# Three moves at the border between layer 1 and the recurrence of a four-layer graph network

## The chip, the cores and the metric

The kernel runs on one core of one Trainium2 chip. The metric is the device time of one execution in microseconds (us): the median of several runs. Below, PE is the matmul engine (TensorE), DVE is VectorE, ACT is ScalarE, POOL is GpSimd and SP is SyncE. SP computes nothing: it issues DMA transfers, one queue for all of them. POOL computes and issues transfers as well, in a queue of its own. Each engine works through its instructions in the order in which they stand.

## The reference, cut to what matters

Sixteen graphs of 1024 nodes with 256 features pass four layers, each of the form `x = x + layer(relu(layernorm(x)), adj)`. Layer 0 is an attention layer, layer 1 a graph convolution, layer 2 a gated recurrence over the nodes, layer 3 a two-layer perceptron on sums over neighbours. Layer 2 is what the change leads up to:

```python
def step(h, i):
    x = jnp.take(h_e, i, axis=1)
    row = jnp.take(norm_adjT, i, axis=1)
    x_par = jnp.einsum('bj,bjd->bd', row, h)
    iou = x @ W_ioux.T + b_ioux + x_par @ W_iouh.T + b_iouh
    r, z = jnp.split(iou, 2, axis=1)
    r, z = (jax.nn.sigmoid(r), jax.nn.sigmoid(z))
    hc = jnp.tanh(x @ W_coux.T + b_coux + x_par * r @ W_couh.T + b_couh)
    h_new = z * x_par + (1.0 - z) * hc
    h = jax.lax.dynamic_update_slice(h, h_new[:, None, :], (0, i, 0))
    return (h, None)
h_out, _ = jax.lax.scan(step, h_e, jnp.arange(n))
```

Node `i` takes the states of all other nodes, those before it already new. So the 1024 steps are sequential in principle. There are two biases for each gate, one with `x` and one with `x_par`; only their sum matters.

## The kernel before, in words

**Layers 0 and 1** (`layers_0_1`) run in one loop over the 16 graphs (line 639). Iteration `i` does layer 0 of graph `i` and layer 1 of graph `i - 1`, and in small helper functions (`a0` to `a6`, `d0` to `d6`), called between the big matrix products, everything that must be ready for the next graph: loads (`load_x`, `get`), stores (`keep`), moments, copies. For all five engines the order of the instructions is the order in which they are written (`tc.manual_schedule`, line 267). At the end of an iteration `late_norm` (line 791) makes `he`, the normalised input of layer 2, and stores it on SP; the next iteration begins with SP's load of `x` for the graph after next.

**Jobs** prepare layer 2 during these iterations, one for each graph (class `Job`, line 485). Inside a tile of 128 nodes the nodes are put into an order in which groups of 16 depend little on one another. A job loads the adjacency near the diagonal and the first column of tiles (`load`: `ad` at line 504 and `ab` at 506, both issued on SP), masks them (`mask`, POOL, lines 517 and 519), turns `he` into feature-major order (`turn`, stored to `heT_d` by POOL at 541), sums the first tile's contributions (`first`, PE line 547), puts the adjacency into the new order (`order`, PE 558 and 560, stored to `near_d` and `next_d` by POOL at 568 and 569), and stores the sums (`base`, to `base_d`, 578). `scale` (524, 525) multiplies by inverse degrees on POOL. The jobs of graphs 14 and 15 come after the loop (lines 806 to 835). Job 15 uses the same tile `ad` as job 13, so its load has to wait for job 13's `order`.

**The recurrence** (`layer_2`, line 852) goes over eight tiles `t` of 128 nodes and in each over eight groups `s` of 16. On PE, DVE, ACT and POOL the written order holds there too (line 1195). Before the first group it needs: the weights `wx` and `wh`, the biases, `he` of tile 0 in feature-major order for all graphs (`load_he`, line 989, issued on SP at 993 in pieces for graphs 0 to 13, 14 and 15), the base sums `bxt` (line 1202), and the reordered adjacency rows of the group, which POOL gathers from `near_d` with an indirect DMA (`Sub.__init__`, line 1008). `Sub.behind` and `Sub.own` spread the gathered rows by products on POOL (1024, 1015).

`Gates(he, s)` (line 1028) copies the group's input to `hs` on POOL (two instructions, line 1034) and makes tasks of the three gate products with `wx` (PE, 1043), whose results get the bias on their way out of PSUM (ACT 1051 for the first, DVE 1048 for the others). For group 0 the tasks are run before the loop. For group 1 they go to the list `todo` of group 0 and are put between its steps by `fill`, which compares the tasks' estimated costs with the share of the step that is over. Two of the three gates come ahead of the first product of the recurrence (`round_`, PE line 1097). Behind them in the list are the base sums of the next tile (`base_tasks`; PE 928, their loads on SP at 895 and 901, their mask on POOL at 906), which need POOL once more.

In the setup ahead of the loop the order on POOL is therefore: the two copies for group 0, the two gathers, four products, and only then, inside group 0, the two copies for group 1 and the gathers of the next group:

```python
he = load_he(0)
gx = Gates(he, 0)
sub = Sub(0, 0)
```

```python
if s == 0:
    gx_next = gx_ahead or Gates(he, 1)
```

For later tiles the copies for group 1 are already made in the last group of the tile before (line 1315), as `gx_ahead`.

**Layer 3** follows, graph by graph (`layer_3`).

Of the kernel before, what the change touches and what calls it, by code (L numbers as in the profile page):

```python
# [9 lines left out]
F32 = mybir.dt.float32  # L10
# [6 lines left out]
P = 128  # L17
B, N, D, H = 16, 1024, 256, 1024
NT = N // P
DC = D // P  # L20
# [22 lines left out]
def gnn_stack(ctx: ExitStack, tc: tile.TileContext, a: dict, out: bass.AP):  # L43
    nc = tc.nc
    const = ctx.enter_context(tc.tile_pool(name="const", bufs=1))
# [25 lines left out]
    table = [const.tile([P, G2, NT, NS], mybir.dt.int32, name=f"table{k}") for k in range(2)]  # L71
    place = const.tile([P, NT * B], F32, name="place")
    dinv = const.tile([P, B, NT], F32, name="dinv")

    def rows(ap):
        return ap.rearrange("(t p) d -> p t d", p=P)
# [187 lines left out]
    def layers_0_1():  # L264
        with ExitStack() as st:
            ET = mybir.EngineType
            st.enter_context(tc.manual_schedule(engines={ET.PE, ET.DVE, ET.Activation, ET.Pool, ET.SP}))
            wp = st.enter_context(tc.tile_pool(name="w01", bufs=1))
# [4 lines left out]
            x, q, h1, h2, g, dis, mean, rs_of, ags = {}, {}, {}, {}, {}, {}, {}, {}, {}  # L273
# [52 lines left out]
            class Moments:  # L326
# [7 lines left out]
                def first(self, tiles):  # L334
                    junk = psum.tile([P, 512], F32, name="pt")[:, :D]
                    for t in tiles:
                        nc.scalar.activation(junk, self.x[:, t], AF.Identity, accum_out=self.sum[:, t : t + 1])
# [13 lines left out]
            def normed(h, x, shift, scale, tiles):  # L351
                for t in tiles:
                    nc.scalar.activation(h[:, t], x[:, t], AF.Relu, bias=shift[:, t : t + 1], scale=scale[:, t : t + 1])
# [235 lines left out]
            def side(us):  # L589
                while later:  # L590
                    later.popleft()()
                left[0] += us * 1.25
                while left[0] > 0:
                    cost = next(math, None)
                    if cost is None:
                        break
                    left[0] -= cost
                left[0] = min(left[0], 0.0)
# [38 lines left out]
            job15 = Job(15, {"hT": "h1", "ao": "q"})  # L637

            for i in range(B):
# [162 lines left out]
                if ahead:  # L802
                    left_of, first, second = combos(q[i + 1])
                    first()
                side(5.0 if run_a else 3.0)
            h2[14] = big.tile([P, NT, D], F32, name="h2", bufs=2)
            normed(h2[14], x[14], m2.shift, m2.rs, all_)
            nc.sync.dma_start(rows(he_d[14]), h2[14])
# [10 lines left out]
            run_b.order()  # L819
            run_b.base()  # L820
            job14.scale()
            h2[15] = big.tile([P, NT, D], F32, name="h2", bufs=2)
            normed(h2[15], x[15], shift, rs, all_)
            nc.sync.dma_start(rows(he_d[15]), h2[15])
            job15.load()
            job14.first()
            job14.turn()
            job14.base()
# [23 lines left out]
    def layer_2(shared, early):  # L852
        with ExitStack() as st:
            wp = st.enter_context(tc.tile_pool(name="w2", bufs=1, reuse_waits="tile"))
# [6 lines left out]
                nc.sync.dma_start(t[:, :, 2 * D :], a[co].rearrange("(c p) e -> p c e", p=P))  # L861
            load_w(wx, "W_iouxT", "W_couxT")

            bias = wp.tile([P, 3, DC], F32, name="bias")
            bias2 = wp.tile([P, 3, DC], F32, name="bias2")
            with nc.allow_non_contiguous_dma(reason="biases, once"):
                for t, io, co in ((bias, "b_ioux", "b_coux"), (bias2, "b_iouh", "b_couh")):
                    nc.sync.dma_start(t[:, :2].rearrange("p q c -> p (q c)"), a[io].rearrange("(k p) -> p k", p=P))
                    nc.sync.dma_start(t[:, 2], a[co].rearrange("(c p) -> p c", p=P))
            nc.vector.tensor_add(bias, bias, bias2)  # L870

            own = wp.tile([P, GB], F32, name="own")
            nc.vector.tensor_reduce(own, ident.rearrange("p (b j) -> p b j", b=GB), AX.X, ALU.add)
# [115 lines left out]
            def load_he(t):  # L989
                he = big.tile([P, DC, B, P], F32, name="he")  # L990
                for b0, b1 in parts if t == 0 else ((0, B),):
                    for c in range(DC):
                        nc.sync.dma_start(he[:, c, b0:b1], heT_d[b0:b1, :, c, t * P : (t + 1) * P].rearrange("b p i -> p b i"))
                return he
# [199 lines left out]

            with tc.manual_schedule(engines={mybir.EngineType.PE, mybir.EngineType.DVE, mybir.EngineType.Activation, mybir.EngineType.Pool}):
                he = load_he(0)
                gx = Gates(he, 0)
                sub = Sub(0, 0)
                bxt = shared.tile([P, DC, B, P], F32, name="bxt")
                for b0, b1 in parts:  # L1200
# [9 lines left out]
                gx.seed_r()  # L1210
                gx.seed_zc()

                near = gx_ahead = None
                behind = []
                for t in range(NT):
                    if t == NT - 1:
# [9 lines left out]
                    for s in range(NS):  # L1226
# [15 lines left out]
                        else:  # L1242
# [8 lines left out]
                            while any(lists):  # L1251
                                i = max(range(2), key=lambda i: len(lists[i]) / max(sizes[i], 1))
                                if s < 5 and share and 6 <= len(todo) < 10:

                                    i = 1
# [15 lines left out]
                        for c in range(DC):  # L1271
                            to = x[:, c].rearrange("p (b i) -> p b i", b=B)
# [16 lines left out]
                        for k, (i0, i1) in enumerate(steps):  # L1289
# [19 lines left out]
                            if k == 0:  # L1309
                                gx_now, gx = gx, gx_next  # L1310
                                if s > 0 and sub_next:
                                    nc.gpsimd.tensor_copy(tick, rx[:, DC - 1].rearrange("p b i -> p (b i)")[:, :1] if K > 1
                                                          else rx[:, DC - 1, :1])
                                    gx = Gates(he if ahead[0] == t else he_next, ahead[1])
                                    gx_ahead = Gates(he_next, 1) if s + 1 == NS else None
# [28 lines left out]
                        near = None  # L1344
                        if s + 1 < NS:
                            near = psum.tile([P, DC, G2 * GR], F32, name="pa")
# [5 lines left out]
                        elif t + 1 < NT:  # L1352
                            next_block(h, sub.bd, 0, False)
                            near = pnx
                            behind = last_tasks(t + 1, bxt_next)
                            bxt, he = bxt_next, he_next
# [67 lines left out]
    def layer_3(shared, x, hn, at, h, eye):  # L1424
        with ExitStack() as st:
# [274 lines left out]
            for b in range(B):  # L1700
# [27 lines left out]
                for k in range(2, 4):  # L1728
                    eps_of((b + 2) * NQ + k)

    layers_0_1()
    with tc.tile_pool(name="shared", bufs=2, reuse_waits="tile") as shared:
        x, hn, at, h = {}, {}, [], {}
        with tc.tile_pool(name="first3", bufs=1, reuse_waits="tile") as first:
            eye = layer_2(shared, early_3(shared, first, x, hn, at, h))
            layer_3(shared, x, hn, at, h, eye)
# [55 lines left out]
```

## Time and profile before

| | |
|---|---|
| median of 3 runs | 4305.25 us (4303.75 to 4311.17) |
| the profiled execution, own time | 4306.4 us |
| its span, first to last instruction | 4304.6 us |
| mean granted clock of PE | 0.982 |
| DMA traffic | 744.72 MB, 173 GB/s on average |
| layers 0 and 1 | until about 1320 us |
| the border: last jobs, setup of the recurrence | about 1320 to 1380 us |
| biases on SP at the border (868, 869) | 1327.66 to 1336.04 us |
| loads of `he` for tile 0 on SP (993) | issued from 1336.34 us |
| first gates on PE (1043) | from 1354.82 us |
| first product of the recurrence on PE (1097) | 1379.63 us |

The profile is of one execution. A line of the timeline gives start, duration, engine, source line, operation, what was written and read, and the number of instructions; in brackets stands the idle time of the engine ahead of the instruction and the one that ended it. PEld are PE's weight loads. SPq is SP's DMA queue: its times are those of issuing a transfer, not of the transfer. "DMA share" is the mean busy share of the 16 DMA engines; with many transfers at once it can read a little above 1.

### The profile page before, as it was taken

How to read it: one execution, taken by the hardware profiler on the slowest of the kernel's cores; microseconds unless marked ns; L12 is line 12 of the kernel's file. 1: busy time of each engine (PE TensorE's matmuls, PEld its weight loads, DVE VectorE, ACT ScalarE, POOL GpSimd, SP SyncE). 2: the span in 40 equal slices, each digit the busy share in tenths (PEclk: the TensorE clock that was granted, in tenths of full speed). 3: DMA queues.
4: the chain of work that ended last, by engine and by line, in shares of the span. 5: the costliest groups of instructions: out<-in, count | busy, mean ns of one | idle time of the engine just before them, and what ended most of it. 6: DMA issues, size and time to landing. Idle time of an engine off the chain costs nothing. (4 is left out here: it accounts for less than half of the span.)

```text
span 4304.6 us, 56454 instructions
## 1 busy us (share of the span) xinstructions
PE 4045.7 (94%) x19307; PEld 2805.0 (65%) x19307; DVE 2677.6 (62%) x6293; ACT 1554.8 (36%) x3907; POOL 1643.0 (38%) x1740
## 2 busy tenths in 40 slices
PE   7999999999997999999999999998799999999998
PEld 3545455555555888888888888877466565665656
DVE  7888987578763434443444444454477777877776
ACT  3454545444432222222222222223233433333332
POOL 2232323434334333232333333333535446364552
PEclk9999999999999999999999999999799999999999
DMA  6666657998767363546364545441443434434320
GB/s 231 209 224 226 215 203 259 266 301 293 266 222 247 123 195 121 188 128 194 122 198 131 185 140 177 145 139 39 158 170 118 150 125 137 157 118 157 122 103 20
DMA packets 406702, 744.72 MB, mean 173 GB/s; under 512 B 75168, under 2 KB 325664, under 8 KB 365344
## 3 DMA queue, kind: packets, MB, share of 16 engines
q1 hardware_dynamic: 370976, 613.49, 41.8%
q0 software_dynamic: 26080, 109.21, 8.9%
q10 hardware_dynamic: 9216, 16.78, 1.1%
q8 instruction: 210, 3.44, 0.3%
q14 instruction: 220, 1.80, 0.1%
HBM read 538.85 MB, written 183.76 MB: 168 GB/s over the span
## 5 line engine op out<-in xcount | busy, mean ns | idle before, releaser
L86 POOL TENSOR_TENSOR rs<-rs_v,mhalf 128x8 f32<-128x8 f32 (+1 forms) x65 | 112.3, 1727 | 932.1 <-DVE rs_v L82 720.4
L928 PE MATMUL pf<-hb,ab 128*128 128x256 f32 x1568 | 416.7, 384 | 7.5 <-DMA hb<-hs_d 7.5
L1043 PE MATMUL pf<-hs,wx 128*128 128x256 f32 x1536 | 346.8, 382 | 15.5 <-POOL hs L1034 13.5
L1043 PEld LDWEIGHTS pf<-hs,wx 128*128 128x128 f32 x1536 | 292.9, 192 | 58.5 <-POOL hs L1034 14.6
L1342 POOL DMA_INDIRECT hs_d<-h,table x128 | 129.0, 1008 | 510.7 <-ACT gates L1051 451.1
L1570 POOL TENSOR_TENSOR ss<-ss,sq 128x512 f32<-128x512 f32 x224 | 298.9, 1350 | 22.8 <-ACT sq L1568 16.7
L928 PEld LDWEIGHTS pf<-hb,ab 128*128 128x128 f32 x1568 | 272.4, 191 | 45.9 <-issue 9.9
L418 PE MATMUL pmm<-w,ag 128*128 128x256 f32 x1024 | 244.9, 394 | 26.1 <-DVE x L421 12.5
L1048 DVE TENSOR_TENSOR gates<-pf,bias 128x512 f32<-128x512 f32 x128 | 88.4, 692 | 289.0 <-PE pf L1043 289.0
L1633 PEld LDWEIGHTS po<-w,hh 128*128 128x128 f32 x2048 | 239.0, 194 | 16.6 <-issue 11.0
L418 PEld LDWEIGHTS pmm<-w,ag 128*128 128x128 f32 x1024 | 197.1, 196 | 76.3 <-DVE x L421 28.5
L1633 PE MATMUL po<-w,hh 128*128 128x128 f32 x2048 | 243.1, 278 | 1.4 <-ACT hh L1616 0.7
L1079 PE MATMUL pf<-bd,h 128*128 128x384 f32 (+4 forms) x512 | 188.8, 458 | 38.1 <-DVE bxt L1082 31.0
L1568 ACT ACTIVATE sq<-hh 128x512 f32<-128x512 f32 x224 | 141.2, 631 | 197.9 <-POOL ss L1570 119.6
L1516 PE MATMUL ph<-bxt,hb 128*128 128x512 f32 x440 | 199.8, 600 | 3.2 <-ACT hb L1488 1.8
L1141 ACT ACTIVATE r<-pr 128x128 f32<-128x128 f32 (+2 forms) x256 | 57.9, 278 | 384.3 <-PE pr L1097 379.3
L1082 DVE TENSOR_TENSOR bxt<-bxt,pf 128x384 f32<-128x384 f32 (+4 forms) x256 | 127.8, 501 | 86.4 <-PE pf L1079 84.6
L1566 DVE SCALAR_TENSOR_TENSOR hh<-ph,b,u 128x512 f32<-128x512 f32 x192 | 141.2, 749 | 46.6 <-PE ph L1562 36.3
L1616 ACT ACTIVATE hh<-hh,rw 128x512 f32<-128x512 f32 x256 | 158.7, 708 | 24.3 <-DVE hh L1615 24.3
L1158 DVE TENSOR_TENSOR w<-w,hc 128x128 f32<-128x128 f32 (+2 forms) x256 | 75.5, 295 | 139.8 <-ACT hc L1157 139.8
L1615 DVE TENSOR_TENSOR hh<-hh,po 128x512 f32<-128x512 f32 x256 | 154.3, 679 | 2.9 <-PE po L1612 2.9
L345 ACT ACTIVATE pt<-x,m_neg 128x256 f32<-128x256 f32 x240 | 114.3, 476 | 108.6 <-DVE m_neg L340 102.3
(363 smaller groups left out, 9238.0 us busy)
## 6 DMA issues: line engine op xcount, KB each, us to landing
at<-in_quarters SPq DMA_DIRECT2D x94, 1024.0 KB, 10.9
t_d<-at SPq DMA_DIRECT2D x64, 1024.0 KB, 10.7
ab<-in_columns SPq DMA_DIRECT2D x127, 512.0 KB, 3.5
bxt<-t_d SPq DMA_DIRECT2D x42, 1024.0 KB, 4.9
bxt<-in_quarters SPq DMA_DIRECT2D x34, 1024.0 KB, 4.8
at<-at POOLq DMA_DIRECT2D x30, 1024.0 KB, 10.5
at<-t_d SPq DMA_DIRECT2D x22, 1024.0 KB, 4.8
pc<-in_own ACTq DMA_DIRECT2D x64, 256.0 KB, 7.2
```

The source lines that it names most:

```text
L418: nc.tensor.matmul(po[:, t - t0], ag[:, c, t * P : (t + 1) * P], w[:, c], start=c == 0, stop=c == DC - 1)
L928: nc.tensor.matmul(pb, ab[:, jts[k]], hb[:, jts[k]], start=k == 0, stop=k == len(jts) - 1)
L1043: nc.tensor.matmul(pg[:, e], wx[:, c, q * D + e * P : q * D + (e + 1) * P], self.hs[:, c], start=c == 0, stop=c == DC - 1)
L1079: nc.tensor.matmul(pf, h[:, g, c * P : (c + 1) * P], bd[:, g, b0 : b0 + n, S : S + far], start=True, stop=True)
L1342: nc.gpsimd.indirect_dma_start(out=hs_d[t][g][:, :], out_offset=row(1, g, t, s), in_=h[:, g], in_offset=None)
L1516: nc.tensor.matmul(pa, st[left][:, k], at[q % 6][:, k], start=onto is None and k == 0, stop=k == 3, skip_group_check=True)
L1566: behind3[:] = [nc.vector.scalar_tensor_tensor(hh[q][:, k], ph, b1[:, k : k + 1], u, op0=ALU.add, op1=ALU.add)]
L1568: nc.scalar.activation(sq, hh[q][:, k], AF.Square)
L1570: nc.gpsimd.tensor_tensor(ss[q], ss[q], sq, ALU.add)
L1615: nc.vector.tensor_mul(hh[q][:, k], hh[q][:, k], pr)
L1616: nc.scalar.activation(hh[q][:, k], hh[q][:, k], AF.Silu, scale=rw[:, k : k + 1])
L1633: nc.tensor.matmul(po[:, n], left[:, c, n * P : (n + 1) * P], right[:, c], start=onto is None and n == 0 and c == 0, stop=c == HH - 1, ski ...
```

## The change

Three things are moved; no arithmetic is added or removed.

- Job 15's two loads (`job15.load()`) stand ahead of graph 15's `normed` and the store of its `he`, instead of behind them.
- The four loads of biases and the addition that joins them move from the start of `layer_2` into layers 0 and 1: the loads to the end of iteration 3, the addition on DVE to the end of iteration 5. The two tiles, 6 numbers per partition each, now belong to the pool that lasts for the whole kernel, which lies below all others.
- `Gates(he, 1)`, that is the two POOL copies for group 1, is called directly behind `Gates(he, 0)` and so ahead of the gathers of `Sub(0, 0)`. Group 0 then takes it as `gx_ahead`; its matmuls stay where they were.

```diff
+    bias, bias2 = (const.tile([P, 3, DC], F32, name=name) for name in ("bias", "bias2"))
...
                 side(5.0 if run_a else 3.0)
+                if i == 3:
+                    with nc.allow_non_contiguous_dma(reason="biases, once"):
+                        for to, io, co in ((bias, "b_ioux", "b_coux"), (bias2, "b_iouh", "b_couh")):
+                            nc.sync.dma_start(to[:, :2].rearrange("p q c -> p (q c)"), a[io].rearrange("(k p) -> p k", p=P))
+                            nc.sync.dma_start(to[:, 2], a[co].rearrange("(c p) -> p c", p=P))
+                if i == 5:
+                    nc.vector.tensor_add(bias, bias, bias2)
...
             job14.scale()
+            job15.load()
             h2[15] = big.tile([P, NT, D], F32, name="h2", bufs=2)
             normed(h2[15], x[15], shift, rs, all_)
             nc.sync.dma_start(rows(he_d[15]), h2[15])
-            job15.load()
...
-            bias = wp.tile([P, 3, DC], F32, name="bias")
-            bias2 = wp.tile([P, 3, DC], F32, name="bias2")
-            with nc.allow_non_contiguous_dma(reason="biases, once"):
-                for t, io, co in ((bias, "b_ioux", "b_coux"), (bias2, "b_iouh", "b_couh")):
-                    nc.sync.dma_start(t[:, :2].rearrange("p q c -> p (q c)"), a[io].rearrange("(k p) -> p k", p=P))
-                    nc.sync.dma_start(t[:, 2], a[co].rearrange("(c p) -> p c", p=P))
-            nc.vector.tensor_add(bias, bias, bias2)
...
                 he = load_he(0)
-                gx = Gates(he, 0)
+                gx, gx_ahead = Gates(he, 0), Gates(he, 1)
                 sub = Sub(0, 0)
...
-                near = gx_ahead = None
+                near = None
```

## The prediction

> **What bounds the kernel now.** I began with the list of busy engines and the forty slices. TensorE (PE) is busy for 94% of the span, and its slices show 9 nearly everywhere. The exceptions include one 7 in the thirteenth slice, which is 1291 to 1399 us: the border between layers 0 and 1 and the recurrence. PE is the bound elsewhere, so only a pause of PE there can be won.
>
> ```profile
> PE 4045.7 (94%) x19307; PEld 2805.0 (65%) x19307; DVE 2677.6 (62%) x6293; ACT 1554.8 (36%) x3907; POOL 1643.0 (38%) x1740
> PE   7999999999997999999999999998799999999998
> ```
>
> Then I read the border in order of time, engine by engine. The columns are start, duration, engine and line, and in brackets the idle time before the instruction with what ended it.
>
> ```profile
> 1322.18 0.38 SPq L824 DMA_DIRECT2D he_d<-h  x1
> 1322.65 0.77 SPq L504 DMA_DIRECT2D ad<-in_near  x1
> 1323.47 1.38 SPq L506 DMA_DIRECT2D ab<-in_columns  x1
> ...
> 1337.10 5.61 PE L547 MATMUL pt<-h,ab 128*128 128x256 f32 x16 [6.24 <-POOL ab L519]
> ```
>
> Job 15's loads wait in SP's queue behind the store of `he` (L824), which waits for ACT. Job 15's first product then waits 6.24 us for `ab`. The tile that the loads write was free earlier: its last reader on PE began at 1318.54 and took 0.27 us.
>
> ```profile
> 1352.23 0.92 POOL L568 DMA_DIRECT2D near_d<-q  x1 [1.22 <-DVE own L873]
> 1354.37 0.81 POOL L1034 COPY hs<-he 128x256 f32<-128x256 f32 x2
> 1363.12 1.09 POOL L1008 DMA_INDIRECT aj<-near_d,table  x1 [7.93 <-DMA next_d<-q]
> 1369.18 3.75 POOL L1024 TENSOR_TENSOR bd<-aj,own 128x1024 f32<-128x1024 f32 x2 [3.69 <-DMA aj<-near_d,table]
> 1373.69 0.73 POOL L1034 COPY hs<-he 128x256 f32<-128x256 f32 x2
> 1354.82 7.02 PE L1043 MATMUL pf<-hs,wx 128*128 128x256 f32 x24 [3.82 <-POOL hs L1034]
> 1363.39 1.02 PE L1209 MATMUL pc<-wx,ident 128*128 128x512 f32 x2
> 1374.14 5.87 PE L1043 MATMUL pf<-hs,wx 128*128 128x256 f32 x16 [9.72 <-POOL hs L1034]
> ```
>
> The second `hs` copy needs only `he`, yet it stands on POOL behind the gather (L1008) and four products. PE waits 9.72 us for it, then runs two gates and starts the recurrence's first product (L1097) at 1379.63. Last, the DMA shares in stretches (the share and GB/s close each line):
>
> ```profile
> 1318.00:1338.00 20.00, 10.18 (x57) 7.94 (x58) 5.38 (x9) 6.93 (x14) 10.16 (x13) 0.90 1.04 388
> 1338.00:1340.00 2.00, 2.00 (x6) 1.55 (x6) 0.00 (x0) 0.00 (x0) 0.00 (x0) 0.50 0.84 132
> 1340.00:1364.00 24.00, 16.88 (x73) 12.13 (x71) 6.36 (x13) 4.26 (x8) 9.99 (x13) 0.91 1.11 328
> 1364.00:1383.00 19.00, 9.28 (x32) 7.47 (x32) 1.48 (x4) 2.64 (x4) 8.92 (x12) 0.73 1.10 317
> 1383.00:1391.00 8.00, 7.47 (x35) 6.24 (x34) 1.65 (x4) 1.95 (x6) 0.00 (x0) 1.00 0.01 2
> ```
>
> The DMA engines are full from 1318 to 1383. Reordering transfers here brings some forward and pushes others back; only bytes or time taken out of the stretch bring the last one forward.
>
> **What the Trainium skill says.** "DMA: Bandwidth & Descriptors", section "Queues, rings and completion order": an engine alternates between queues packet by packet. The trace agrees, since POOL's stores and SP's loads progress together here. The same page, "Rules for kernel authors": a load with a non-contiguous last dimension becomes one descriptor per element. The trace shows it: 1680 packets under 512 B from 1334 to 1340, for biases of 2 x (512 + 256) = 1536 elements. "TensorE: Matmul & The Clock Gate", Part 1, "What's actually happening": after some 3.4 us of idling PE runs at half clock for about as long. The trace has a granted clock of 0.50 from 1370 to 1378, after the 9.72 us wait.
>
> **The change, part by part.**
>
> **The copies ahead of the gather.** Two POOL copies (0.73 us together, no DMA) move past two gathers and four products. They fall into POOL's 7.93 us wait, so they delay the gather by nothing; without that cover it would be 0.73 us. PE's 9.72 us go. The two gates behind them then run warm: a later 24 of these matmuls take 5.34 us, so 16 take 3.6 instead of 5.87, 2.2 us less. Sum 11.9 us; L1097 could start at 1367.7. Next late would be its operands. `x` was ready at 1366.4. `wh` went out at 1359.5 to 1360.6, and the `ab` load right behind it landed 6.4 us after 1360.62, so `wh` is in by 1367.0. Neither binds.
>
> **Job 15's loads ahead of the store.** Two SP issues (0.77 and 1.38 us) go out at 1318.8 instead of 1322.65, 3.85 us earlier. The added wait, on PE, ends 3.4 us before the store's data is ready, so the store and `wx` behind it in SP's queue lose nothing. They also pass the 1.1 MB that POOL stored at 1320.0 to 1322.5. SP's and POOL's 3.0 MB then in flight at 388 GB/s take 7.8 us from about 1321, so `ab` lands near 1329.5, not 1336.7. L547 then waits only for the transposes ahead of it on PE, which end at 1330.9: it starts at about 1331.1, 6.0 us earlier, and warm (3.7 us as at 1319.5, not 5.61), 1.9 more. Job 15's stores on POOL go out 7.9 us earlier, at 1344.3, and the gather at about 1355.2.
> PE does not get 7.9 us. Its first gates need `he`, whose last pieces went out at about 1346 and landed in 6.2 to 7.4 us, at 1352.5. The transfers ahead of it are the same but for the biases (minus 1.7 us, below), and of the 1.94 MB that jobs 14 and 15 store, about half now runs ahead of it (0.95 MB at 360 GB/s, plus 2.6). I estimate `he` at 1353.3 and its copy at 1353.4, 1.0 us earlier than 1354.37. Bounds: 2.1 us later if all the stores pass it, 4.4 earlier if none does.
>
> **The biases.** SP loses four issues at the border, 0.57 + 4.34 + 0.55 + 2.78 = 8.2 us. That was hidden, as DMA was full throughout. What counts is the dip of 1338 to 1340: 2.0 us at 132 instead of 388 GB/s, worth 1.3 to 2.0 us; I take 1.7, for everything queued later. In iteration 4 of layers 0 and 1 the four issues stand ahead of the load of `x` (now 322.9) and three quarter loads. By SP's 8.2 and the dip's 2.0 us, `x` comes up to 10.2 us later; by the four shortest issues (4 x 0.55) and 1.3, 3.5 us. ACT first reads it at 335.70 without a wait:
>
> ```profile
> 335.70 0.40 ACT L337 ACTIVATE pt<-x 128x256 f32<-128x256 f32 x1
> 346.63 0.48 ACT L345 ACTIVATE pt<-x,m_neg 128x256 f32<-128x256 f32 x1 [4.82 <-DVE m_neg L340]
> ```
>
> ACT idles 1.85 and 4.82 us before 346.63, so a delay up to 6.7 us is covered; beyond, `m_neg` is late on DVE, PSUM reads queue behind it, and at most 3.5 us reach PE. DMA had paused just before 323 and SP idles after its last issue there, so I take the short end: 0 us. The quarters are first used after 360. The 0.10 us add on DVE costs nothing measurable; it leaves the border too.
>
> **What is late next.** The 11.9 and 1.0 us put L1097 at 1366.7 and the step's end 12.9 us earlier. The loads for batch 2 of the base then bind. They follow everything queued, which ends at 1382.5 minus 1.7; 1.44 MB at 360 GB/s (4.0 us) and about 1 us to land give 1385.8. PE first uses them at 1398.44, less 12.9: 1385.5. Minus 0.3 us. The mask for batch 0 stands on POOL behind the next gather; with the gather at 1355.2 it is done by 1370, and PE wants it at 1374.4. Unmoved it would be 1376.1 and cost 1.7.
>
> Sum: 11.9 + 1.0 - 0.3, about 12.5 us. The profiled execution took 4306.4 us, of which 4304.6 are the span; I expect a span near 4292.1 and 4293.9 in all. From the median of 4305.25 it is 4292.8.
>
> **Rivals.** First, DMA takes most back. All of job 14's and 15's stores pass `he` (2.1 us late instead of 1.0 early), PE stays cold through the second gates (2.2), and mask or batch 2 costs 1.5: 11.9 - 2.1 - 2.2 - 1.5 = 6.1 us, 4299.2. For it speaks that DMA is full; against, that the 9.72 us wait has nothing to do with DMA.
> Second, slower: a new wait at a reused buffer. The bias tiles move to the pool below all others, and the recurrence's tiles shift against those of job 15. If `he` came to lie on `q`, which job 15's last stores read, its load would wait for them (up to 1362.3 as now), and then 2.1 MB at 290 GB/s, 7.2 us, and 1 us: `he` at 1370.5. Gates and set-up (7.0 + 2.7 + 3.6) put L1097 at 1384.1, 4.5 us later than now: 4309.8. It decides once those stores land after about 1358. Against it: now `he` is loaded before `q` is even written, so the tiles are apart, and the shift is small (48 bytes per partition).
> Third, nothing at the border but the full 3.5 us loss in iteration 4: 11.9 + 1.0 - 0.3 - 3.5 = 9.1, 4296.2.
> That the copies are not moved can be left out: POOL follows the written order in both stages, SP in layers 0 and 1.
>
> **How the numbers follow.** Forecast 0.62, loss in iteration 4 0.08, DMA takes it back 0.22, new wait 0.05, the rest unnamed 0.03. The range reaches from 4288 (`wh` alone as the limit: now in by about 1364 at the earliest, so L1097 at 1362.3) to 4299.5. A difference of 0.2%, 8.6 us, is about what a measurement of this kernel can tell from no change. Forecast and third rival lie beyond it, the first and most of the second within: faster 0.68, same 0.27, slower 0.05.
>
> **What would show it.** In the changed trace: no bias load at the border; `ab` landed by 1331 and L547 not waiting 6 us; four L1034 copies together before L1008; L1043 with no gap after L1209; L1097 near 1366.7, at full clock. It is wrong if PE stands before L1097, L928 or the first gates for a DMA, or if the stretch from 322.4 to 393.3, one iteration of layers 0 and 1 by SP's stores of `he`, takes over 72 us instead of 70.9.

## The result and the profile after

| | before | changed |
|---|---|---|
| median of 20 runs each | 4307.07 us (4296.36 to 4315.53) | 4299.49 us (4291.69 to 4311.28) |
| ratio, 95% interval | 1 | 0.9984 [0.9977, 0.9992] |
| the profiled execution, own time | 4306.4 us | 4295.2 us |
| its span, granted clock of PE | 4304.6 us, 0.982 | 4293.4 us, 0.984 |

The change is worth 0.16%, 6.9 us (3 to 10), where 12.5 us were forecast: faster, but by about half, and less than the 8.6 us that the prediction took for the least difference that can be told from none. I read the border first, as before. Line numbers of the changed kernel are one higher than before inside layer 2 and the jobs (L1097 is now L1098, L928 L929, L1034 L1035, L901 L902).

The page's busy list and PE's slices, as of before:

```profile
PE 4042.0 (94%) x19307; PEld 2797.7 (65%) x19307; DVE 2674.9 (62%) x6293; ACT 1554.7 (36%) x3907; POOL 1644.1 (38%) x1740
PE   7999999998997999999999999998799999999998
```

PE has 3.7 us less work by its records, and the 7 in the thirteenth slice stays. So PE still pauses at the border. The border in order of time, first SP's queue and what it feeds:

```profile
1318.88 0.33 SPq L505 DMA_DIRECT2D ad<-in_near  x1
1319.26 0.92 SPq L507 DMA_DIRECT2D ab<-in_columns  x1
1322.21 0.38 SPq L833 DMA_DIRECT2D he_d<-h  x1
...
1333.44 5.36 PE L548 MATMUL pt<-h,ab 128*128 128x256 f32 x16
1348.31 0.92 POOL L569 DMA_DIRECT2D near_d<-q  x1 [1.22 <-DVE own L874]
1350.45 1.50 POOL L1035 COPY hs<-he 128x256 f32<-128x256 f32 x4
1359.26 1.09 POOL L1009 DMA_INDIRECT aj<-near_d,table  x1 [7.31 <-DMA next_d<-q]
```

Job 15's loads stand ahead of the store of `he` (L833), no bias follows, and L548 no longer waits for `ab`. The four `hs` copies stand together ahead of the gather, and `he` was there when POOL came to them. Then PE:

```profile
1350.91 6.90 PE L1044 MATMUL pf<-hs,wx 128*128 128x256 f32 x24 [3.82 <-POOL hs L1035]
1359.36 1.02 PE L1210 MATMUL pc<-wx,ident 128*128 128x512 f32 x2
1360.22 3.62 PE L1044 MATMUL pf<-hs,wx 128*128 128x256 f32 x16
1364.26 1.97 PE L1098 MATMUL pr<-x,wh 128*128 128x256 f32 x8 [0.43 <-DMA wh<-in_W_iouhT]
...
1388.66 1.19 PE L929 MATMUL pf<-hb,ab 128*128 128x256 f32 x2 [4.51 <-DMA hb<-he_d]
...
1393.49 2.57 PE L1098 MATMUL pr<-x,wh 128*128 128x256 f32 x8
```

The same places before:

```profile
1379.84 1.89 PE L1097 MATMUL pr<-x,wh 128*128 128x256 f32 x8
...
1398.44 0.60 PE L928 MATMUL pf<-hb,ab 128*128 128x256 f32 x2
...
1400.81 1.89 PE L1097 MATMUL pr<-x,wh 128*128 128x256 f32 x8
```

The 9.72 us wait is gone and the two gates run warm, that is at full clock. The recurrence's first product comes at 1364.26 instead of 1379.84, 15.6 us earlier (the 1379.63 of the prediction is the start of its weight load). Then the bracket at L929 shows a wait that the kernel before did not have: 4.51 us for `hb` of batch 2, which is graph 2 of the base sums for the next tile. The second group's first product came at 1400.81 before and comes at 1393.49 now, so 7.3 us are left. It runs partly at half clock (2.57 us for what took 1.89), and 6.7 us are left at the group's first scatter, the indirect store of new states to `hs_d`, before and after:

```profile
1416.02 1.02 POOL L1342 DMA_INDIRECT hs_d<-h,table  x1 [0.16 <-issue]
```

```profile
1409.36 1.02 POOL L1343 DMA_INDIRECT hs_d<-h,table  x1 [0.16 <-issue]
```

The waits of PE between 1318 and 1400 confirm it (total, times, longest):

```profile
PE pf L929 <- DMA hb<-he_d: 4.5, 1, 4.5
PE pf L1044 <- POOL hs L1035: 3.8, 1, 3.8
```

What releases batch 2's loads is seen in SP's queue:

```profile
1362.86 0.70 SPq L902 DMA_DIRECT2D hb<-he_d  x1
1363.66 9.40 SPq L994 DMA_DIRECT2D he<-heT_d  x2
1373.24 5.66 SPq L965 DMA_DIRECT2D ao<-next_d  x3
1378.95 1.13 SPq L1390 DMA_DIRECT2D eps<-in_epsilon  x1
1380.19 0.37 SPq L896 DMA_DIRECT2D ab<-in_columns  x1
1380.60 1.42 SPq L902 DMA_DIRECT2D hb<-he_d  x1
```

Batch 2 takes over the buffers of batch 0, whose products PE began at 1372.99, so they were free some 3 us later (e4, below, shows the 3.3 us). But `he` and `ao` of tile 1 stand ahead in the queue, their issue alone takes 15 us, and batch 2's loads go out at 1380.2. Before, they went out at 1390.80, 10.3 us after the last issue ahead of them (1379.15 and 1.39 us): then the buffers set the pace, now the queue does. Last, the stretches of before:

```profile
1318.00:1338.00 20.00, 14.45 (x69) 11.68 (x70) 5.40 (x9) 6.96 (x14) 10.26 (x13) 0.83 1.04 394
1338.00:1340.00 2.00, 1.44 (x10) 1.00 (x8) 0.11 (x1) 0.47 (x1) 0.00 (x0) 1.00 1.06 348
...
1364.00:1383.00 19.00, 15.95 (x74) 12.47 (x75) 6.25 (x13) 6.16 (x14) 7.68 (x8) 1.00 1.10 314
1383.00:1391.00 8.00, 3.48 (x16) 2.54 (x15) 1.36 (x3) 0.40 (x1) 5.59 (x8) 0.81 0.98 315
```

The dip of 1338 to 1340 is filled (348 instead of 132 GB/s). PE does 15.95 us of work from 1364 to 1383 instead of 9.28, and is busy for only 3.48 of the next 8 us, where before it was busy for 7.47. There the DMA engines now move 315 GB/s, and moved 2 before: PE has come forward, the last transfers have not.

The two profiled executions lie 11.2 us apart, more than the border gives. The rest arises in the recurrence: from the second group's first scatter to the last scatter it took 1624.1 us before and 1618.7 after, and in all eighteen traces of this study between 1618.7 and 1630.5, in no order that goes with an edit. It goes with the granted clock: over this stretch PE stood at half clock for 53.9 us before and 42.6 after, in all eighteen for 42.5 to 63.6, and the stretch is 0.46 us longer for each of these us (correlation 0.84). The largest piece is 10.2 us from 1607.2 in the kernel before, at the border to tile 1, where the changed kernel has none. So a single profile tells where a wait is, and only the timed runs tell what it is worth.

### The profile page after: what moved, and what is told of

Read it like the earlier page. It is cut to its first block, busy times and chain, and to the rows that moved or that the text cites. A ratio compares the mean times of both kernels' runs of the same rounds, so it can differ in the third digit from the quotient of the medians.

```text
span 4293.4 us, 56453 instructions
## 1 busy us (share of the span) xinstructions
PE 4042.0 (94%) x19307; PEld 2797.7 (65%) x19307; DVE 2674.9 (62%) x6293; ACT 1554.7 (36%) x3907; POOL 1644.1 (38%) x1740
## 5 line engine op out<-in xcount | busy, mean ns | idle before, releaser
L929 PE MATMUL pf<-hb,ab 128*128 128x256 f32 x1568 | 417.0, 384 | 11.1 <-DMA hb<-hs_d 6.5
L929 PEld LDWEIGHTS pf<-hb,ab 128*128 128x128 f32 x1568 | 272.3, 191 | 50.4 <-issue 14.8
```

Source lines behind the costliest of these rows:

```text
L929: nc.tensor.matmul(pb, ab[:, jts[k]], hb[:, jts[k]], start=k == 0, stop=k == len(jts) - 1)
```

## The experiments

Theories: **A**, batch 2's loads come too late in SP's queue and give back at the border what the copies win. **S**, the two bias tiles in the lowest pool shift all tiles above them by 64 bytes per partition (two times 32; the prediction said 48), off the multiples of 256, and their transfers become slower. **P**, the bias loads cost time by their place in iteration 3. "Border" below is the time from SP's last store of layer 1's output (L812 before, 1312.54 us) to the recurrence's first product and to the second group's first scatter, so that differences of the kernel's start drop out: 67.3 and 103.5 us before, 51.7 and 96.8 after.

| kernel | median, us | of before on the same chip, us | ratio [95%] | border, us |
|---|---|---|---|---|
| e1 copies alone | 4293.94 | 4303.54 | 0.9979 [0.9971, 0.9987] | 57.7, 94.0 |
| e2 job 15 alone | 4298.85 | 4303.54 | 0.9991 [0.9984, 0.9997] | 61.0, 97.2 |
| e3 biases alone | 4310.19 | 4303.54 | 1.0020 [1.0012, 1.0028] | 68.0, 104.1 |
| e4 all, batch 2 first | 4297.14 | 4303.54 | 0.9985 [0.9977, 0.9992] | 51.9, 88.2 |
| f1 copies and job 15 | 4296.10 | 4305.86 | 0.9976 [0.9969, 0.9983] | 54.7, 92.4 |
| f2 biases at the start | 4311.89 | 4305.86 | 1.0012 [1.0004, 1.0021] | 69.9, 106.1 |
| f3 tiles alone | 4311.09 | 4305.86 | 1.0007 [1.0000, 1.0014] | 67.8, 103.9 |
| f4 = f1, batch 2 first | 4292.41 | 4305.86 | 0.9962 [0.9948, 0.9976] | 52.1, 88.3 |
| g1 all, 256 aligned | 4299.67 | 4309.55 | 0.9977 [0.9970, 0.9983] | 50.9, 94.0 |
| g2 biases, 256 aligned | 4307.88 | 4309.55 | 1.0002 [0.9994, 1.0010] | 66.5, 102.7 |
| g3 all, aligned, batch 2 first | 4298.19 | 4309.55 | 0.9975 [0.9966, 0.9984] | 51.4, 87.7 |
| g4 = g3, job 15 in another buffer | 4300.80 | 4309.55 | 0.9985 [0.9978, 0.9992] | 60.6, 96.8 |
| h1 = f4 and 64 unused bytes | 4296.42 | 4305.69 | 0.9975 [0.9968, 0.9982] | 54.1, 90.5 |
| h2 = f4 and 256 unused bytes | 4290.90 | 4305.69 | 0.9971 [0.9959, 0.9983] | 54.2, 90.4 |
| h3 = before and 64 unused bytes | 4313.04 | 4305.69 | 1.0015 [1.0008, 1.0022] | 67.2, 103.4 |
| h4 = before and 256 unused bytes | 4304.29 | 4305.69 | 0.9996 [0.9986, 1.0005] | 67.9, 104.0 |

The ratio is the one on record for repeated timings and not the quotient of the two medians; with few runs the two differ (f4: 0.9962 and 0.9969). None of these kernels leaves out or changes a part of the computation.

**Each part alone (e1, e2, e3).** The kernel before with one move each; e1's edit:

```diff
-                gx = Gates(he, 0)
+                gx, gx_ahead = Gates(he, 0), Gates(he, 1)
...
-                near = gx_ahead = None
+                near = None
```

> The kernel before with the third move alone: both pairs of hs copies ahead of the first gather; job 15's loads and the biases stay where they were. Points of comparison in the profile: the start of the recurrence's first product (1379.8 us before, 1364.3 with all three moves) and the first scatter of the second group (1416.0 before, 1409.4 with all three, so 6.7 us kept of 15.6). Theory A, the loads of batch 2 of the base sums set the pace: SP is busy until about 1380.5 with the loads of he, ao and eps, so hb of batch 2 lands at about 1388.5 whatever PE does. The first product comes at 1367.7 (11.9 us earlier, 3.6 us later than with all three), PE reaches batch 2 at about 1386.5 and waits 2 us[...]: 9 to 10 us kept at the scatter, more than the whole change keeps. Rival B, what is lost is a fixed cost of the moved copies or of the second group itself: the loss is again 8 to 9 us, so 3 to 4 us kept.

> The kernel before with the first move alone: job 15's two loads ahead of the store of he. Theory A: job 15's stores go out 3.9 us earlier, as with the whole change, the gather and the second hs copies follow, the first product is 3.9 us earlier, batch 2 is in time, and all 3.9 us are kept at the second group's scatter. PE's wait of some 9.7 us ahead of the two gates stays. Step of the prediction: 7.9 us earlier, at the stores and at the first product alike. Rival: nothing is kept, because the reordered loads push other transfers back: 0 to 1 us.

> The whole change with the first and the third move undone: only the biases are loaded in iteration 3 and added in iteration 5. Theory A: the biases hid behind POOL's chain; the first product moves by less than 1 us, and nothing is kept or lost in layers 0 and 1 (each iteration's store of he within 0.3 us of before). The prediction's step: whatever is queued behind them comes 1.7 us earlier, without a gain for PE as long as POOL is last. Rival: the issues in iteration 3 delay the load of x so that PE loses up to 3.5 us there.

Measured: 0.9979, 0.9991 and 1.0020, that is 9.0 and 3.9 us won by the first two and 8.6 us lost by the biases alone. The sum of the three would be 4.3 us won; all together gave 6.9. At the border e2 won 6.3 us at both places, between the 3.9 of theory A and the 7.9 of the prediction's step: its stores went out 4.7 us earlier (1348.24), and the wait ahead of the two gates shrank to 5.13 us instead of staying. PE in the kernel with the copies alone:

```profile
1368.89 1.89 PE L1097 MATMUL pr<-x,wh 128*128 128x256 f32 x8
...
1387.65 0.60 PE L928 MATMUL pf<-hb,ab 128*128 128x256 f32 x2
...
1390.02 1.89 PE L1097 MATMUL pr<-x,wh 128*128 128x256 f32 x8
```

By the border's measure it starts the recurrence 6.0 us later than the whole change does (57.7 against 51.7), and its second group scatters 2.8 us earlier (94.0 against 96.8). The first product came some 2.5 us later than expected, as the first gates began 1.3 us later and ran longer at half clock (8.20 us instead of 7.02 before), and so the 2 us wait that was expected did not occur. L928 finds `hb` loaded, so PE neither waits nor falls to half clock. That is what A says: in the three kernels where PE waits for it, `hb` of batch 2 lands 74.6 to 76.1 us after the store from which the border is counted (after, f1, g1), and a start that is too early for that only buys a wait. In f1, which starts between the two, the wait is 0.56 us. The loss of e3 is not at the border (68.0 and 104.1 against 67.3 and 103.5), which A leaves unexplained.

**Batch 2 first (e4).** SP's loads for tile 1 are issued behind those of batch 2:

```diff
+                    mark[b] = nc.sync.dma_start(hb[:, t:], rows(he_d[b])[:, t:])
...
-                                he_next = load_he(t + 1)
+                                with tc.issue_after(mark[2].ins) if t == 0 else nullcontext():
+                                    he_next = load_he(t + 1)
...
-                            behind = last_tasks(t + 1, bxt_next)
+                            with tc.issue_after(mark[2].ins) if t == 0 else nullcontext():
+                                behind = last_tasks(t + 1, bxt_next)
...
-                        eye = next(early)
+                        with tc.issue_after(mark[2].ins):
+                            eye = next(early)
```

> The whole change, and on SP the loads of he for tile 1, of ao and hr for tile 1 and the early loads of layer 3 are issued behind the loads of batch 2 instead of ahead of them (an order on SP alone; nothing waits for data). Theory A: ab and hb of batch 2 go out at about 1376.5, when PE lets go of batch 0, and land by about 1383; PE's wait of 4.5 us for hb and the 2.5 to 3 us at half clock behind it are gone. The first product stays at 1364.3; at the second group's scatter 13.5 to 14.5 us are kept instead of 6.7, and the kernel is 13 to 14 us below the one before. Rival B, the loss has another cause than these transfers (the mask on POOL, the clock, the second group's own chain): 6.7 us kept, as with the whole change. Rival C, the loads put off come too late for tile 1: the gain shows in the second group and is gone by the first group of tile 1 (1609 us).

SP's queue and PE in this kernel, whose layers 0 and 1 ended 3.2 us later by its start:

```profile
1378.74 0.34 SPq L898 DMA_DIRECT2D ab<-in_columns  x1
1379.18 0.38 SPq L905 DMA_DIRECT2D hb<-he_d  x1
1379.60 5.72 SPq L999 DMA_DIRECT2D he<-heT_d  x2
...
1386.38 0.60 PE L934 MATMUL pf<-hb,ab 128*128 128x256 f32 x2
```

The mask's load for batch 2 goes out 3.3 us after the first products of batch 0 began (1375.48), `hb` behind it and ahead of `he`. PE does not wait for it, and the second group's scatter stands 15.3 us earlier than before (88.2 against 103.5) where the whole change had 6.7. `hb` landed at 1385.50, 69.7 us after the store from which the border is counted, instead of 76.1. So A is shown for the border: the order in SP's queue took 8.6 us of what the copies and job 15 had won. The timed ratio did not follow: 0.9985 against 0.9984. The loads that were put off are not late, as rival C had it: up to the first scatter of tile 1 e4 still keeps 13.4 us and the whole change 6.9, and the 1.9 us that e4 lost on the way go with 3.4 us at half clock, which f1 and g1, without this order, have as well. Then PE waits for `hr`. This place in e4, then after:

```profile
1597.50 3.73 PE L984 MATMUL pf<-ao,hr 128*128 128x112 f32 x16 [2.34 <-DMA hr<-hs_d]
```

```profile
1600.82 2.01 PE L979 MATMUL pf<-ao,hr 128*128 128x112 f32 x16 [2.31 <-DMA hr<-hs_d]
```

The wait is the same, and in e4 PE fell to half clock behind it, for 10.2 us, as in the kernel before; after the next group 13.6 us are kept in e4 and 11.4 in the whole change. Whether it does differs between traces of like kernels (f4 did, g3 did not). Over the whole recurrence the six kernels with this order stood at half clock for 52.1 us on average and the twelve others for 51.9. So in this trace the clock takes the gain back (58.6 us against 42.6 in the whole change), but the order is not shown to be the cause of that.

**Where the biases cost (f1 to f4).** f1 is the change without its bias move; f2 loads the biases at the kernel's start; f3 is the kernel before with only the two tiles moved, loads and addition left at the border; f4 is f1 with e4's edit. f3's edit:

```diff
+    bias, bias2 = (const.tile([P, 3, DC], F32, name=name) for name in ("bias", "bias2"))
...
-            bias = wp.tile([P, 3, DC], F32, name="bias")
-            bias2 = wp.tile([P, 3, DC], F32, name="bias2")
```

> The kernel before with the first and the third move; the biases stay at the border, in their old pool. The biases alone measured 1.0020 of the kernel before in repeated timings, while their one profile shows nothing lost. Theory P (place): the loads in iteration 3 cost about 8 us in most executions. Theory S (shift): it is the two tiles in the lowest pool, which move every other tile by 48 bytes. Theory N (noise of these timings): neither. With P or S this kernel is faster than the whole change, by up to 8 us: 4 to 12 us below the kernel before, ratio 0.997 to 0.999. With N it lies at the whole change's 0.9984. In the profile, theory A (batch 2's loads behind he, ao and eps): the first product 15 us earlier or a little less, PE waits for hb of batch 2 for 3 to 5 us, and 5 to 8 us are kept at the second group's scatter, less than the 10.8 us that the copies alone keep.

> The kernel before with the bias tiles in the lowest pool and their loads at the start of layers 0 and 1, behind the load of the second x, instead of at the border or in iteration 3. Theory P: the cost of iteration 3 is gone, 0.9990 to 1.0005 of the kernel before. Theory S: 1.002, as with the loads in iteration 3.

> The kernel before with the two bias tiles in the lowest pool and nothing else: loads and addition stay at the border. Theory P: equal to the kernel before within 0.05%. Theory S: 1.002. Theory N: equal.

> First and third move, biases as before, and the loads of he, ao and hr for tile 1 and layer 3's early loads behind those of batch 2 on SP. Theory A: as with the whole change and this order, PE does not wait for hb; 11 to 13 us are kept at the second group's scatter. With P or S the kernel is 11 to 14 us below the one before (0.9968 to 0.9975), with N 7 us, as the whole change with this order.

Without the bias move the change gives 0.9976, 10.3 us. Biases loaded at the start cost as well (1.0012), and so, barely, do the tiles alone (1.0007), though all their loads are at the border: iteration 3 is not needed for the loss, which speaks against P and for S. Both lie between the forecasts of the two theories, so neither settles it. In the profile f1 missed its forecast (a wait of 3 to 5 us, 5 to 8 us kept): it waits 0.56 us and keeps 11.1. f4 is the fastest here, from six runs.

**Off and on multiples of 256 bytes (g1 to g4).** An unused tile of 192 bytes behind the bias tiles makes the shift 256 bytes:

```diff
+    nc.vector.memset(const.tile([P, 48], F32, name="pad"), 0.0)
```

> The whole change and, behind the two bias tiles, an unused tile of 192 bytes (set to zero once), so that the tiles of layers 0 and 1 move by 256 bytes instead of 64. In the kernel before, the large tiles of layers 0 and 1 start at multiples of 256 bytes; in the four kernels profiled with the bias tiles in the lowest pool they start 64 behind one, and there SP's queue shows 50.4 to 50.7% of the DMA engines for the same bytes between 100 and 1300 us instead of 49.7 to 49.8%. Theory S (shift): that share is back at 49.8% and the kernel is 10 to 13 us below the one before, ratio 0.9970 to 0.9977; the biases' place in iteration 3 costs nothing. Theory P (place): the share falls, but the ratio stays at the whole change's 0.9984.

> The biases alone moved to iteration 3 (1.0020 of the kernel before), with the same unused tile of 192 bytes. Theory S: 0.9995 to 1.0005 and a share of SP's queue of 49.8%. Theory P: 1.002 again.

> The whole change, the unused tile of 192 bytes, and the loads of he, ao and hr for tile 1 and layer 3's early loads behind those of batch 2 on SP. Theory A and S together: no wait for hb, 13 to 15 us kept at the second group's scatter, and 13 to 16 us below the kernel before, 0.9963 to 0.9970; it is then the fastest so far, with or a little below the kernel without the biases' move (0.9962). If the loads put off are late for tile 1, it stays at 0.9975.

> As the last, and job 15 turns he into a tile of its own (a quarter's buffer free since the last sums) instead of the one that job 13's stores still read. Early loads for job 15 slow those stores: in the changed kernel ACT waits 5.3 us for them, and job 15's first product starts at 1333.4 instead of the 1331.1 of the prediction and runs 5.4 us instead of 3.7. Theory: that wait goes, job 15's stores go out 3 to 4 us earlier (1344.5 instead of 1348.3), but the first product then waits for wh, which cannot land much before 1364: the gain over the last kernel is under 1.5 us. Rival: everything moves up by the 4 us.

The biases alone go from 1.0020 to 1.0002, and the whole change from 0.9984 to 0.9977, where the intervals overlap. g3 kept 15.7 us at the second group's scatter, more than was expected, but its ratio stays at that of g1, 0.9975 against 0.9977, and missed the forecast. g4 missed too: the first product came 9.2 us later than in g3. Its edit gives job 15 another piece of memory for one tile:

```diff
-        job15 = Job(15, {"hT": "h1", "ao": "q"})
+        job15 = Job(15, {"hT": "at3", "ao": "q"})
```

What SP waited for between 1318 and 1372, and then its queue and POOL:

```profile
SPq L869 <- DMA heT_d<-at: 15.9, 1, 15.9
```

```profile
1323.29 0.38 SPq L834 DMA_DIRECT2D he_d<-h  x1
1339.67 0.38 SPq L869 DMA_DIRECT2D wx<-in_W_iouxT  x1
...
1359.47 1.43 POOL L1041 COPY hs<-he 128x256 f32<-128x256 f32 x4 [11.33 <-DMA he<-heT_d]
```

The memory of `at3` is where `wx` goes, so SP stood 15.9 us for job 15's store, and `he` and all else behind it. This is the mechanism of the prediction's second rival, a wait at a reused buffer in front of SP's queue; it came by my edit and not by the change.

**The shift by itself (h1 to h4).** The kernel before, and the fastest kernel f4, each with an unused tile of 64 or of 256 bytes in the lowest pool and nothing else:

```diff
     dinv = const.tile([P, B, NT], F32, name="dinv")
+    nc.vector.memset(const.tile([P, 16], F32, name="pad"), 0.0)
```

> The first and third move with batch 2's loads brought ahead of the pieces for tile 1, the biases where they were, and one unused tile of 64 bytes per partition in the lowest pool, so that all tiles above stand 64 bytes off. Nothing of the computation is left out. If the shift costs time by itself, this is 3 to 8 us (0.1 to 0.2%) slower than the same kernel with 256 unused bytes, and 1 KB packets of layers 0 and 1 take 51 ns on average instead of 49. If not the shift but the moved bias loads cost, both are the same within 0.1% and near 0.9962 of the kernel before.

> As the last, but with 256 unused bytes instead of 64: the tiles stand at multiples of 256 bytes again. If the shift costs: 0.996 to 0.997 of the kernel before, 3 to 8 us faster than with 64 bytes. If the 0.9962 of the kernel without any unused tile was luck of few runs: near 0.9976, what the two moves gave without the reordered loads.

> The kernel before with 64 unused bytes in the lowest pool and nothing else. If the shift costs time by itself: 1.0007 to 1.002 of the kernel before, 3 to 8 us. If it doesn't: 1.000.

> The kernel before with 256 unused bytes in the lowest pool. If only the distance to multiples of 256 bytes matters: 1.000 of the kernel before, within 0.0007. If any other place of the tiles costs: above 1.0007, like the one with 64 bytes.

On the kernel before, 64 bytes cost 0.15% and 256 bytes nothing: 1.0015 against 0.9996, with intervals apart. On the fastest kernel the medians lie 5.5 us apart in the same direction, but the intervals overlap (0.9975, 0.9971; seven runs of the second), so whether f4's 0.9962 was luck of six runs stays open. On the kernel before S is shown: the shift alone costs time, with no bias moved, some 3 to 8 us (f3, h3, and e3 against g2). Only shifts by 64 and by 256 bytes were run. The cost is not paid at the border, where h1 stands with h2 and h3 with h4. The queue's share of the DMA engines between 100 and 1300 us (packets, MB, share), in the kernel before, with 64 and with 256 bytes:

```profile
q1 hardware_dynamic: 116897, 216.29, 49.7%
```

```profile
q1 hardware_dynamic: 116918, 216.46, 50.6%
```

```profile
q1 hardware_dynamic: 116904, 216.35, 49.7%
```

Nearly the same packets and bytes hold the engines 0.9 points of 49.7 longer. By size, packets of 1 KB before 1310 us took 51 ns on average in every kernel with the 64 byte shift (seven traces) and 49 in every other (eleven). "DMA: Bandwidth & Descriptors", section "How a descriptor splits into AXI transactions", says that each transaction must start at a multiple of 256 bytes, and that a descriptor that does not begin there fetches bytes from the boundary below it. From that page an estimate for 1024 bytes at 64 past a boundary is 34 beats of 32 bytes instead of 32, 6% more; 4% were measured. For 8 KB it is 258 beats instead of 256, 0.8% more; between 100 and 1300 us these packets took 381 ns instead of 378. Packets of 2 KB, for which it would be 3%, took the same in both groups (93 ns), which is not explained.

How the longer packets become the end of the kernel some us later, I could not show. From the first to the last store of `he` in layers 0 and 1 the seven shifted traces took 1146.1 us on average and the eleven others 1144.7, 1.4 us less, with a spread of 1.4 and 0.8 us in the groups; the rest is not seen in single profiles.

## Why the prediction was partly right and came out wrong

- **The copies ahead of the gather: right.** The 9.72 us are gone, and the second gates take 3.62 us as forecast (3.6). L1098 waits 0.43 us for `wh`, at 1364.26, which the prediction had taken as in by 1367.0. Alone, the copies gave 9.0 us in the timed runs, at the border 9.5 of the 11.9.
- **Job 15's loads: right in direction, mis-sized.** `ab` is masked at 1330.17 (landing forecast for 1329.5), so the wait for it is gone. But L548 begins at 1333.44 instead of 1331.1 and cold, 5.36 us instead of 3.7. The early loads share the engines with job 13's stores of `next_d`, and ACT's copy into the tile that these read waited for them, as the waits of ACT show: the store of `next_d` from 1321.0 took 9.9 us to land, and 6.1 before. So job 15's stores go out 3.9 us earlier (1348.31), not 7.9. PE's first gates came 3.9 us earlier all the same (1350.91), not 1.0: `he`, which was estimated for 1353.3 and was to hold them, was in before POOL asked for it at 1350.45. Two sizes were off in opposite directions; that the term came out above its forecast is luck. The wait of ACT, then the mask of `ab`:

```profile
ACT h L539 <- DMA next_d<-h: 5.3, 1, 5.3
```

```profile
1330.17 0.29 POOL L520 TENSOR_SCALAR_AFFINE_SELECT ab<-ab 128x128 f32<-128x128 f32 x1 [0.76 <-DMA ab<-in_columns]
```

- **Sum up to L1098: 15.6 us against 12.9 forecast.** From the first gates to L1098 it is 13.35 us now and was 25.02, 11.7 won of the 11.9; job 15's 3.9 instead of 1.0 makes the difference. The loss against the forecast does not come from here.
- **What is late next: the step that failed.** The prediction named the right wait, batch 2 of the base, even as a sign by which it would be wrong, and priced it at 0.3 us. From the first product to the second group's scatter 15.6 - 6.7 = 8.9 us were lost in the profile: 1.1 by 1382.10 (L1350, at 1396.55 before, 14.45 us earlier), 4.5 in the wait, 2.6 in the matmuls behind it up to 1393.49 and 0.7 after. It had the loads land at 1385.8: all that is queued ahead comes 1.7 us earlier, and then their bytes go at 360 GB/s. They landed at 1388.6. SP issued the last piece of `ao` until 1378.9, only 0.2 us earlier than before, and `hb` from 1380.6 to 1382.0, and from 1382 to 1388 the engines moved 289 GB/s. And PE wanted them at 1384.15, not 1385.5, as it was earlier. Behind the wait PE ran at half clock, which the prediction counted for the 9.72 us and not here. Moving the loads ahead of `he` (e4) removes the wait. In the timed runs this term is not clear of noise: without the bias move 0.9976 becomes 0.9962 or 0.9971, 2 to 6 us, with it nothing (e4) or 1 us (g3 against g1), and all intervals overlap.
- **The biases' shift: the second step that failed, named and not priced.** The prediction called it small and asked only whether tiles come to overlap. By the ratios it costs some 3 us in the whole change (0.9984 against 0.9977 with the tiles aligned, or 0.9976 without the move; the intervals overlap), and 3 to 8 us on the kernel before, where it is shown. The 6.7 us left at the border do not contain it, so it is partly chance that they are so near the 6.9 us of the timed runs.
- **The biases in iteration 4: right.** `x` is issued at 326.94, 4.0 us later than 322.9 and inside the bounds of 3.5 to 10.2. ACT reads it at 335.45 without a wait, and SP's stores of `he` stand at 322.17 and 393.00, 70.8 us apart as before. The third rival did not occur. The filled dip was worth about its 1.7 us at the border, where the other two moves are made as well: the four kernels with the bias move (after, e4, g1, g3) start the recurrence 50.9 to 51.9 us after the store, the four without (f1, f4, h1, h2) 52.1 to 54.7, on average 2.3 us later. In three of these POOL waits 2.4 to 4.4 us for `he` in its copies (f1, f4, h2), with the move at most 0.9. In the timed runs it is not seen: the shift, which comes with it, costs more, and with the tiles aligned the bias move alone neither won nor lost (g2, 1.0002).

```profile
326.27 0.57 SPq L811 DMA_DIRECT2D bias<-in_b_couh  x1
326.94 0.41 SPq L279 DMA_DIRECT2D x<-in_x  x1
...
335.45 0.39 ACT L338 ACTIVATE pt<-x 128x256 f32<-128x256 f32 x1
```

- **The rivals.** The first, that DMA takes most back, ends nearest to the measured time (6.1 us, against 6.9), but not by its way: `he` was not late and the second gates not cold. Of its terms only batch 2 came, larger. The second rival did not occur.

With both failed terms out of the way, batch 2 first and no shift, two of the three moves run at 0.9962 and 0.9971 (f4, h2; six and seven runs), 12 to 16 us, the size of the forecast. That is the version to keep. What stays open: how much of the border's 8.6 us from batch 2 is kept on average, since g3 and e4 show next to nothing of it and f4 and h2 some of it. That batch 2 costs the 4.5 us wait is shown; that it is what made the timed gain half of the forecast is not.

## What to carry to other kernels

Price the next wait with the same care as the one you remove: follow its loads to the place in the issuing queue where they stand and ask what is issued ahead of them. Here a load whose buffer was free at about 1376.3 went out at 1380.2, behind 15 us of issuing. A new small tile in a pool that lies below the others moves every buffer above it; keep such additions at multiples of 256 bytes (64 bytes cost 0.15% here, 256 nothing). Undo each part of a compound change alone, as a part that costs can hide behind one that wins.

## What was not expected of the hardware

- Sixty-four unused bytes at the bottom of the memory made the kernel before 0.15% slower, and 256 did not; 1 KB packets took 51 ns instead of 49.
- Single executions of one kernel lie up to 16 us from its median, and this goes with the mean granted clock (0.978 to 0.985, lower clock, longer time).
- A wait of 2.3 us for `hr` at the same place left PE at full clock in one trace (2.01 us for sixteen matmuls) and at half clock in another (3.73 us).
